# Row sums of a fourth of the attention heads: from matrix multiplications to accumulating transfers, with a reordered program

## The chip, the core and the metric

The kernel runs on one core of a Trainium2 chip. The core has five engines that work side by side, each through its own list of instructions in order: PE (TensorE, matrix multiplications), DVE (VectorE), ACT (ScalarE), POOL (GpSimd) and SP (SyncE, which here only starts transfers). They meet by semaphores: an instruction waits until what it reads is written and what it overwrites is no longer read. 16 DMA engines carry transfers, which POOL and SP start. The metric is the device time of one launch in microseconds (us).

## What is computed

The reference is two graph layers over 32 graphs of 512 nodes with 256 features, 8 heads of 32, everything in float32:

```python
# layer 0, then layer 1 without the feed-forward part; x is (32, 512, 256)
allowed = (adj > 0) | (adj.T > 0) | eye            # layer 1: adj != 0 alone
q, k, v = heads(x @ Wq.T + bq), heads(x @ Wk.T + bk), heads(x @ Wv.T + bv)
attn = softmax(where(allowed, q @ k.T / sqrt(32), -inf))
y = layernorm(x + (attn @ v) @ Wo.T + bo)          # layer 0
y = layernorm(y + relu(y @ W1.T + b1) @ W2.T + b2) # layer 0
x = layernorm(x + y)
```

The kernel does not subtract a row maximum. It computes p = exp(s) times the 0/1 mask, the product of p with v, and separately the row sum of p over the 512 keys, by whose reciprocal the product is multiplied. How this row sum is made is what the change is about.

## The kernel before, in words

**Layout.** Scores are held transposed, keys on the 128 partitions and queries along the row. The 512 keys are four chunks and the eight heads two head groups `hg` of four, so a layer of a graph has eight tiles `p(layer, k)`, k = 4 hg + chunk, each 128 x 4 heads x 512 queries. `scores(layer, k)` (L472) is eight small matmuls into the one PSUM tile `s`, `exp` (L487, ACT) turns it into p, `masked` (L490, DVE) multiplies p by the mask, and `product` (L494, PE) adds p times v to the one PSUM tile `acc`, which `context` (L507, ACT) copies to `cT`. Both layers share one `cT`, so `context` also waits for the `project` steps that read the last one.

**Row sums.** For each head group four p tiles are first folded into one, p(layer, 2 + hg):

- `pair(layer, k)` (L510) is an accumulating transfer started by POOL: p(k) += p(k + 1), 1024 KB. There are three in a layer.
- `fold` (L514) is an addition on DVE.

What is left is a sum over the 128 partitions of the folded tile. There are two ways, chosen by the set `SPREAD` (L164):

- `sums` (L517): four matmuls of the tile with a matrix of ones, on PE, into a PSUM bank. DVE then transposes the result in blocks (`blocks`, L558), takes the reciprocal (`invert`) of one column, transposes it back (`widen`) and multiplies (`divide`).
- spread: two accumulating transfers (`halve`, L536) add the upper half of the partitions to the lower half, 128 to 64 (512 KB) and 64 to 32 (256 KB); four `spread` transfers (64 KB each, started by SP) put the 32 rows of the four heads under each other in a tile `part`; `blocks` transposes `part`, and `reduce` (L566, DVE) adds 32 columns. `part` and its transpose have one buffer each. The rest is as above.

Before, the head groups (0, 0) and (1, 0), written (layer, hg), are spread, and (0, 1) and (1, 1) go over PE. Layer 0 of the first graph and layer 1 of the last are direct (L260): there all eight tiles are summed on PE, with no pair, fold, halve or spread.

**The rest of a graph.** `add`, `stats`, `aggregate` (DVE), `root` (POOL, two instructions), `center`, `affine`, `offset` (DVE) and `norm` (ACT) make the layer norms, numbered 1 to 4. `transpose` and `transpose_out` turn activations; `query_key`, `value`, `project`, `hidden` and `mlp` are dense matmuls, with `*_out` and `relu` on ACT taking them out of PSUM. A dense step is done as four 32-column matmuls side by side ("narrow", 128*32 in the profile) or as one of 128 columns (`wide=True`, 128*128); the values are the same. `flip`, `sort` and `join` bring x in transposed, `cast`, `entries` and `entry` bring the adjacency, `masks` makes the masks of it, and `guard` keeps a running sum of the totals for an overflow test at the end.

**The order.** Nothing is scheduled by a tool. Three lists written out by hand call these steps one by one, and each engine runs its share in that order: `opening` for graphs 0 to 4, `period` called 26 times, each with five consecutive graphs a to e, and `closing` for graphs 27 to 31. In a period, graph b is in its layer 1 attention, c in its layer 0 feed-forward part and norms, d in layer 0 attention, e is being loaded and a finished. Which buffer a tile gets is written out too, as strings of digits in `slots` (L168): three PSUM banks "d" for all dense results, eight buffers "p", and so on.

In the period of before, b.sums(1, 1) stands at L1725 behind d.product(0, 0), and b.blocks(1, 1) and b.invert(1, 1) a few steps behind it; the transfers of (1, 0) follow, with b.project(1, 0) at L1795.

Of the kernel before, what the change touches and what calls it, by code (L numbers as in the profile page):

```python
# [27 lines left out]
def kernel(ctx: ExitStack, tc: tile.TileContext, t: dict, out: bass.AP):  # L28
# [122 lines left out]
    def plain(pools: ExitStack):  # L151
# [7 lines left out]
        def dense(out, lhsT, rhs, start, stop, wide):  # L159

            for at in (slice(0, P),) if wide else [slice(j * HD, (j + 1) * HD) for j in range(HPC)]:
                nc.tensor.matmul(out[at], lhsT[:, at], rhs, start=start, stop=stop)  # L162

        SPREAD = {(0, 0), (1, 0)}  # L164
# [5 lines left out]
                "01201201010202020201212102110212101201202012020212010202102201201201201201011021021021021021102012102102102012012020"  # L170
                + "210212121020212121021021210210012121201202020121202020120120201201102020" * 13
                + "212120102112010201201202120121021101101221121221021202110210210210210120201201210120120120120120221212012012"
            ),
            "p": iter(
                "012345672103456712045673061537245024371652617403253074615261473065073142564213074"
                + "573021654162073153076245124673025073461526143076573014256421073453072165416273015073624512463072573046152614073653071425642173045073216541623071573062451246073253074615261473065073142564213074" * 2
                + "57301625465107352037416251467034273650124015673"
# [8 lines left out]
                + "101010" * 13  # L186
                + "1011101"
            ),
            "y": iter(
                "01230123012310320132013102130232131302312013010132102301"  # L190
                + "303012032130131302312013010132102301" * 8
                + "2003213012300303012301231010210213023102"
# [4 lines left out]
                + "011010100101"  # L197
            ),
            "st": iter(
                "01230132013201320132103213021302132013201203"  # L200
                + "12032103210321031230213021302130" * 13
                + "1203123021032103032103210321032103213021032103213201"
            ),
            "r": iter(
                "0123102101"
                + "31102001" * 13
                + "32212010123110"
# [7 lines left out]
                "01011001"  # L215
                + "1001" * 13
                + "1001"
            ),
            "total": iter(
                "01101"  # L220
                + "1001" * 13
                + "1000101"
# [439 lines left out]
        def opening(a, b, c, d, e):  # L662

            a.load()
            a.constants(0, 4)
            a.warm()
            b.flip(1)
            a.transpose(0, 0)
            a.transpose(0, 1)
            a.transpose_out(0, 0)  # L670
            a.cast(first[0])
            a.constants(22, 23)
            a.transpose_out(0, 1)
            a.query_key(0, 1, 0, None, wide=True)
            a.query_key(0, 0, 0, None, wide=True)
            a.query_key_out(0, 1, 0, None)
            a.query_key_out(0, 0, 0, None)
            a.scores(0, 2)
            a.exp(0, 2)
            a.entries()  # L680
            a.value(0, 1)
            a.scores(0, 1)
            a.exp(0, 1)
            a.query_key(0, 0, 1, None)
            a.query_key_out(0, 0, 1, None)
            a.entry(2)
            a.scores(0, 0)
            a.entry(0)
            a.exp(0, 0)
            a.entry(1)  # L690
            a.value(0, 0)
            a.entry(3)
            a.constants(6, 8)
            b.cast(first[6])
            a.value_out(0, 0)
            b.sort(1, 0, 0)
            a.masks(0)
            a.masks(1)
            a.scores(0, 3)
            a.query_key(0, 1, 1, None)  # L700
            a.masks(2)
            a.masked(0, 0)
            b.flip(0)
            a.masked(0, 2)
            a.constants(4, 6)
            b.sort(1, 0, 1)
            a.masked(0, 1)
            b.sort(1, 1, 0)
            a.exp(0, 3)
            a.masked(0, 3)  # L710
            a.query_key_out(0, 1, 1, None)
            a.scores(0, 4)
            b.sort(0, 0, 0)
            a.value_out(0, 1)
            a.exp(0, 4)
            a.masked(0, 4)
            b.sort(0, 1, 0)
            a.once(2, 0)
            a.once(2, 1)
            a.scores(0, 5)  # L720
            a.once(2, 2)
            a.once(2, 3)
            a.exp(0, 5)
            a.scores(0, 6)
            b.sort(0, 1, 1)
            a.masked(0, 5)
            a.exp(0, 6)
            a.product(0, 0)
            a.product(0, 1)
            a.product(0, 2)  # L730
            a.scores(0, 7)
            b.sort(1, 1, 1)
            a.exp(0, 7)
            b.sort(0, 0, 1)
            b.join(0, 0)
            a.product(0, 3)
            a.sums(0, 0)
            a.once(0)
            b.entries()
            b.join(1, 0)  # L740
            a.context(0, 0)
            b.entry(1)
            b.join(0, 1)
            a.product(0, 4)
            a.constants(12, 14)
            a.masked(0, 6)
            a.product(0, 5)
            a.masked(0, 7)
            a.constants(20, 22)
            a.product(0, 6)  # L750
            a.product(0, 7)
            a.blocks(0, 0)
            a.reduce(0, 0)
            a.constants(8, 10)
            a.sums(0, 1)
            a.constants(17, 20)
            a.once_out(0)
            a.context(0, 1)
            a.bias(1)
            b.join(1, 1)  # L760
# [3 lines left out]
            b.query_key(0, 0, 0, None)  # L764
            b.load()
            b.entry(3)
            c.flip(1)
            b.query_key_out(0, 1, 0, None)
            a.invert(0, 1)
            a.widen(0, 1)  # L770
            a.divide(0, 1)
            b.value(0, 0)
            b.query_key_out(0, 0, 0, None)
            a.invert(0, 0)
            a.widen(0, 0)
            b.entry(2)
            b.scores(0, 0)
            a.divide(0, 0)
            b.value_out(0, 0)
            a.project(0, 0)  # L780
            a.project(0, 1)
            b.exp(0, 0)
            b.scores(0, 1)
            a.add(1, 1)
            a.stats(1, 1)
            a.add(1, 0)
            c.cast()
            a.stats(1, 0)
            a.aggregate(1, 1)
            a.add(1, 3)  # L790
            a.aggregate(1, 0)
            a.once(1)
            a.constants(10, 12)
            b.exp(0, 1)
            a.center(1, 1)
            a.once_out(2)
            a.stats(1, 3)
            b.query_key(0, 1, 1, None, wide=True)
            a.masks(3)
            a.root(1, 0, 2)  # L800
            a.add(1, 2)
            a.stats(1, 2)
            a.affine(1, 1)
            a.center(1, 0)
            a.affine(1, 0)
            b.query_key(0, 0, 1, None, wide=True)
            a.aggregate(1, 2)
            b.query_key_out(0, 1, 1, None)
            a.transpose(1, 0)
            b.entry(0)  # L810
            b.masks(0)
            a.aggregate(1, 3)
            a.center(1, 3)
            b.query_key_out(0, 0, 1, None)
            a.transpose_out(1, 0)
            a.root(1, 2, 4)
            b.scores(0, 2)
            a.hidden(0, 2)
            a.affine(1, 3)
            c.flip(0)  # L820
            a.relu(0, 2)
            a.once_out(1)
            a.hidden(0, 4)
            c.entry(1)
            c.sort(0, 1, 0)
            c.sort(0, 0, 0)
            a.hidden(0, 0)
            a.relu(0, 3)
            b.exp(0, 2)
            c.sort(0, 1, 1)  # L830
            b.masks(1)
            a.relu(0, 4)
            a.relu(0, 5)
            b.masks(2)
            b.scores(0, 3)
            b.exp(0, 3)
            a.center(1, 2)
            a.affine(1, 2)
            b.masked(0, 0)
            a.relu(0, 1)  # L840
            a.transpose(1, 1)
            b.value(0, 1, wide=True)
            b.value_out(0, 1)
            b.bias(1)
            b.masked(0, 2)
            b.scores(0, 5)
            b.masked(0, 1)
            b.product(0, 0)
            b.pair(0, 0)
            b.masks(3)  # L850
            c.join(0, 1)
            a.hidden(0, 6)
            c.sort(1, 1, 0)
            b.exp(0, 5)
            a.relu(0, 0)
            a.guard(0, 0, 1)
            b.masked(0, 3)
            c.entry(2)
            b.masked(0, 5)
            b.product(0, 1)  # L860
            b.product(0, 2)
            b.pair(0, 2)
            a.relu(0, 7)
            a.transpose_out(1, 1)
            a.hidden(1, 2)
            a.bias(0)
            a.relu(0, 6)
            a.mlp(0)
            a.mlp(1)
            a.add(2, 0)  # L870
            a.stats(2, 0)
            a.aggregate(2, 0)
            b.bias(0)
            a.relu(1, 3)
            a.hidden(1, 4)
            a.relu(1, 2)
            c.sort(1, 1, 1)
            c.join(1, 1)
            c.sort(0, 0, 1)
            b.product(0, 3)  # L880
            a.add(2, 1)
            a.stats(2, 1)
# [2094 lines left out]
```

## Time and profile before

| | us |
|---|---|
| median of 3 runs (2986.01 to 2986.1) | 2986.01 |
| the profiled execution | 2986.66 |
| its span, first to last instruction | 2984.9 |
| TensorE clock granted, share of full | 0.999 |
| one of the 26 periods | 91.58 |
| opening, up to the first period's first matmul | 304.7 |
| psR matmuls (all sums), 624 records | 79.8 busy |
| p<-p transfers in the software queue with the mask's | 47.5% of 16 engines' span |

Busy time of an engine is the union of its instructions. A matmul in float32 is two records, and its end is modelled and lies in the next one's time, so the time that a step takes on PE is read from its start to the start of the next. In the tables "x512" is a count, "busy, mean ns" the time of a group, and what stands behind the next bar is idle time of the engine ahead of the group, with what ended it. A tile's name is without its number: psR is a bank of `sums`, acc of `product`, psO of `project`, psF of `mlp`, psH of `hidden`, psT of `transpose`, s of `scores`. L162 is the helper through which all dense matmuls go.

### The profile page before, as it was taken

The numbers are of one execution on the slowest core, as the hardware profiler recorded it, in microseconds if no ns is written. First come the engines' busy times: TensorE is split into PE (matmuls) and PEld (weight loads), VectorE is DVE, ScalarE is ACT, GpSimd is POOL, SyncE is SP. The second block draws the span as 40 slices with busy tenths as digits, with TensorE's granted clock in tenths as the row PEclk, the third lists the DMA queues.
The fourth block names the chain that finished last, engine by engine and source line by source line (L and its number), as shares of the span: only waits on it lengthen the run. The fifth ranks groups of instructions, "written<-read, shape, count | busy, mean of one in ns | idle before, by whom it ended". The sixth has DMA issues, their size and how long they took to land.

```text
span 2984.9 us, 83822 instructions
## 1 busy us (share of the span) xinstructions
PE 2959.3 (99%) x36852; PEld 1369.0 (46%) x36852; DVE 2700.2 (90%) x3585; ACT 1748.9 (59%) x2111; POOL 1002.0 (34%) x1247
## 2 busy tenths in 40 slices
PE   9999999999999999999999999999999999999997
PEld 4444444454444444444544445444445444454443
DVE  5889999999999999999999999999999999998996
ACT  5555665655665556655566555566555665656554
POOL 0333333332333323333323333233332333333332
PEclk9999999999999999999999999999999999999999
DMA  7566766776666667667676766676676766767551
GB/s 174 109 115 129 156 130 134 135 127 137 133 135 135 122 132 147 134 128 136 129 144 127 133 134 130 131 143 131 131 132 128 146 130 133 135 123 141 100 109 29
DMA packets 276436, 387.08 MB, mean 130 GB/s; under 512 B 153248, under 2 KB 237344, under 8 KB 245792
## 3 DMA queue, kind: packets, MB, share of 16 engines
q0 software_dynamic: 35744, 260.59, 47.5%
q1 hardware_dynamic: 240320, 121.05, 18.4%
q8 instruction: 291, 4.77, 0.6%
q14 instruction: 81, 0.66, 0.1%
HBM read 72.23 MB, written 33.55 MB: 35 GB/s over the span
## 4 chain that ended last, share of the span: by engine, by line
PE 95%; DVE 2%; ACT 1%; DMA 1%; issue 0%; POOL 0%; SPq 0%; DVEq 0%; POOLq 0%
PE s L479 18%; PE acc L499 15%; PE psH L162 15%; PE psF L162 15%; PE psQK_None L162 11%; PE psV L162 7%; PE psO L162 7%; PE psQK L162 4%; PE psT L440 2%; PE psR L523 2%; ACT p L488 1%; DMA p<-p 1%; DVE st L606 0%; DVE p L515 0%; DVE y L603 0%
## 5 line engine op out<-in xcount | busy, mean ns | idle before, releaser
L488 ACT ACTIVATE p<-s 128x2048 f32<-128x2048 f32 x512 | 963.6, 1882 | 486.0 <-PE s L479 478.7
L492 DVE TENSOR_TENSOR p<-p,m 128x2048 f32<-128x2048 f32 x512 | 1162.5, 2278 | 29.7 <-ACT p L488 26.5
L479 PE MATMUL s<-qT,kT 32*64 32x512 f32 x8192 | 570.4, 613 | 6.8 <-ACT p L488 2.7
L499 PE MATMUL acc<-p,v 128*32 128x512 f32 x4096 | 507.8, 595 | 0.0
L162 PE MATMUL psH<-xT,w_L_gnn_W 128*32 128x256 f32 (+1 forms) x6296 | 471.0, 380 | 0.0
L162 PE MATMUL psF<-w_L_gnn_W,hT 128*32 128x256 f32 (+1 forms) x6896 | 459.9, 379 | 0.0
L614 POOL TENSOR_SCALAR rs<-mv 128x2 f32<-128x2 f32 (+1 forms) x320 | 215.2, 673 | 684.4 <-DVE mv L609 664.8
L515 DVE TENSOR_TENSOR p<-p,p 128x2048 f32<-128x2048 f32 x186 | 424.3, 2281 | 3.9 <-DMA p<-p 2.7
L162 PEld LDWEIGHTS psH<-xT,w_L_gnn_W 128*32 128x32 f32 (+1 forms) x6296 | 300.3, 118 | 199.5 <-issue 54.7
L615 POOL TENSOR_TENSOR rs<-rs,neg_half 128x2 f32<-128x2 f32 (+1 forms) x320 | 369.8, 1156 | 26.7
L162 PEld LDWEIGHTS psF<-w_L_gnn_W,hT 128*32 128x32 f32 (+1 forms) x6896 | 286.6, 115 | 184.7 <-ACT hT L650 31.4
L512 POOL DMA_DIRECT2D p<-p x186 | 171.3, 921 | 497.8 <-PE acc L499 435.4
L650 ACT ACTIVATE hT<-psH,c_L_gnn_b 128x256 f32<-128x256 f32 x512 | 212.5, 475 | 193.5 <-PE psH L162 184.4
L479 PEld LDWEIGHTS s<-qT,kT 32*64 32x64 f32 x8192 | 119.2, 129 | 313.5 <-issue 109.3
L539 POOL DMA_DIRECT2D p<-p x124 | 106.4, 858 | 443.7 <-DVE mv L609 193.5
L162 PE MATMUL psQK_None<-xT,w_L_gnn_Wqkv 128*32 128x512 f32 (+1 forms) x1988 | 243.1, 594 | 0.7 <-ACT xT L445 0.7
L162 PE MATMUL psO<-w_L_gnn_Wo,cT 128*32 128x256 f32 (+1 forms) x2728 | 240.0, 380 | 2.7 <-DVE cT L585 2.7
L499 PEld LDWEIGHTS acc<-p,v 128*32 128x32 f32 x4096 | 118.7, 109 | 256.7 <-issue 193.0
L162 PEld LDWEIGHTS psO<-w_L_gnn_Wo,cT 128*32 128x32 f32 (+1 forms) x2728 | 154.5, 123 | 97.8 <-issue 43.0
L445 ACT COPY xT<-psT 128x512 f32<-128x512 f32 x130 | 76.1, 586 | 199.4 <-PE psT L440 199.4
L635 ACT ACTIVATE x<-z,ms,rs 128x256 f32<-128x256 f32 x128 | 73.5, 599 | 158.6 <-DVE ms L619 155.4
L606 DVE BATCH_NORM_STATS2 st<-y 128x6 f32<-128x256 f32 x384 | 155.0, 422 | 6.5
(79 smaller groups left out, 2873.9 us busy)
## 6 DMA issues: line engine op xcount, KB each, us to landing
p<-p POOLq DMA_DIRECT2D x186, 1024.0 KB, 7.8
p<-p POOLq DMA_DIRECT2D x62, 512.0 KB, 5.9
x<-in_x_dram SPq DMA_DIRECT2D x32, 512.0 KB, 4.2
code<-in_adj_dram POOLq DMA_DIRECT2D x32, 512.0 KB, 6.3
m<-code SPq DMA_DIRECT2D x32, 512.0 KB, 4.9
kT<-v SPq DMA_DIRECT2D x248, 64.0 KB, 4.0
p<-p POOLq DMA_DIRECT2D x62, 256.0 KB, 5.9
part<-p SPq DMA_DIRECT2D x248, 64.0 KB, 2.0
```

The source lines that it names most:

```text
L162: nc.tensor.matmul(out[at], lhsT[:, at], rhs, start=start, stop=stop)
L479: nc.tensor.matmul(s[half * P // 2 : (half + 1) * P // 2, j, :], self.kT(layer)[at, hg, key : key + P // 2], self.qT(layer)[at, hg, :], st ...
L488: nc.scalar.activation(self.p(layer, k), self.at("s", (layer, k), [HPC, N]), AF.Exp, scale=SCALE)
L492: nc.vector.tensor_tensor(p, p, m[:, k % NQ, None, :].to_broadcast([P, HPC, N]), ALU.mult)
L499: nc.tensor.matmul(acc[j * HD : (j + 1) * HD, :], self.v(layer)[:, kc, h * HD : (h + 1) * HD], self.p(layer, k)[:, j, :], start=(kc == 0), ...
L512: nc.gpsimd.dma_start(out=self.p(layer, k), in_=self.p(layer, k + 1), accum_op=ALU.add)
L515: nc.vector.tensor_tensor(self.p(layer, dst), self.p(layer, a), self.p(layer, b), ALU.add)
L539: nc.gpsimd.dma_start(out=p[:rows], in_=p[rows : 2 * rows], accum_op=ALU.add)
L606: nc.vector.bn_stats(self.at("st", (n, i), [6]), self.y(n, i))
L614: nc.gpsimd.tensor_scalar(rs, self.mv(n)[:, a:b, 1:2], EPS, None, ALU.add)
L615: nc.gpsimd.tensor_tensor(rs, rs, neg_half[:, a:b, None], ALU.pow)
L650: nc.scalar.activation(self.hT(h)[:, f, :], ps[:, f % 2, :], AF.Relu, bias=b1[:, f : f + 1])
```

## The change

1. `SPREAD` gains (1, 1). Layer 1's second head group is now summed by two `halve` and four `spread` transfers and a `reduce`, in all graphs but the last; its `sums` step on PE goes.
2. The period is written in another order: the same steps for the same five graphs, but for item 1, with other neighbours and partly other offsets between the graphs. Five dense steps of the period go from wide to narrow and four from narrow to wide.
3. The opening and the closing are rewritten to lead into the new period and out of it, and the strings of `slots` with them.

The diff, cut to its core, with the new period's steps that the sum of (1, 1) touches:

```diff
-        SPREAD = {(0, 0), (1, 0)}
+        SPREAD = {(0, 0), (1, 0), (1, 1)}
...
         slots = {
             "d": iter(
-                "01201201010202020201212102110212101201202012020212010202102201201201201201011021021021021021102012102102102012012020"
...
+                "01201201212020202021020121012021210120120212210102010121100201201210120120120202202120202010210210210121021021020200"
...
         def period(a, b, c, d, e):
...
-            b.sums(1, 1)
...
-            b.blocks(1, 1)
...
-            b.invert(1, 1)
...
```

The new period around them, other steps left out:

```python
c.halve(0, 0, P // 2)
c.halve(0, 0, P // 4)
c.spread(0, 0, 0)
...
c.fold(0, 3, 3, 4)
c.sums(0, 1)
...
b.masked(1, 0)
b.product(1, 0)
...
a.root(4, 0, 2)
c.blocks(0, 1)
...
c.divide(0, 0)
...
c.project(0, 1)
...
c.project(0, 0)
...
b.context(1, 0)
b.scores(1, 6)
...
b.product(1, 4)
...
b.masked(1, 6)
...
b.pair(1, 4)
c.root(1, 0, 2)
...
c.affine(1, 0)
...
c.center(1, 1)
c.affine(1, 1)
...
c.transpose(1, 0)
c.transpose_out(1, 0)
d.scores(0, 0)
...
b.fold(1, 3, 6, 7)
...
b.fold(1, 3, 3, 4)
...
c.hidden(0, 0)
...
b.halve(1, 1, P // 2)
...
b.halve(1, 1, P // 4)
b.halve(1, 0, P // 2)
...
b.spread(1, 1, 0)
...
b.spread(1, 1, 3)
...
b.spread(1, 1, 1)
b.halve(1, 0, P // 4)
...
d.scores(0, 4)
d.exp(0, 4)
...
b.spread(1, 1, 2)
...
d.masked(0, 4)
...
c.root(2, 0, 2)
...
e.entry(1)
b.blocks(1, 1)
...
b.reduce(1, 1)
...
b.spread(1, 0, 2)
...
b.invert(1, 1)
b.widen(1, 1)
...
b.divide(1, 1)
...
b.blocks(1, 0)
b.reduce(1, 0)
...
b.project(1, 0, wide=True)
...
b.project(1, 1, wide=True)
...
d.scores(0, 7)
d.context(0, 0)
d.product(0, 4)
...
c.scores(1, 2)
```

In the new opening, where graph 0 is still alone on the engines, the steps around the fourth to sixth scores are:

```python
a.scores(0, 3)
...
a.exp(0, 3)
a.value(0, 0)
...
a.scores(0, 6)
...
a.exp(0, 6)
...
a.scores(0, 4)
...
a.product(0, 0)
```

## The prediction

> **What bounds the kernel.** I read the shares of busy time first, then the chain that ended last:
>
> ```profile
> PE 2959.3 (99%) x36852; PEld 1369.0 (46%) x36852; DVE 2700.2 (90%) x3585; ACT 1748.9 (59%) x2111; POOL 1002.0 (34%) x1247
> PE 95%; DVE 2%; ACT 1%; DMA 1%; issue 0%; POOL 0%; SPq 0%; DVEq 0%; POOLq 0%
> ```
>
> PE is the path nearly everywhere, so a step taken from PE is worth its time on PE, unless the new order makes PE wait. Since matmuls overlap, I take a step's cost from start to start. The timeline of PE in one period (start, length, engine, line, tiles, count):
>
> ```profile
> 1169.84 1.04 PE L499 MATMUL acc<-p,v 128*32 128x512 f32 x8
> 1170.81 1.11 PE L479 MATMUL s<-qT,kT 32*64 32x512 f32 x16
> ...
> 1176.49 0.66 PE L440 MATMUL psT<-ident,x 128*128 128x128 f32 x4
> 1176.98 3.62 PE L162 MATMUL psF<-w_L_gnn_W,hT 128*128 128x256 f32 x16
> 1180.53 1.11 PE L479 MATMUL s<-qT,kT 32*64 32x512 f32 x16
> 1181.58 1.07 PE L499 MATMUL acc<-p,v 128*32 128x512 f32 x8
> 1182.46 1.04 PE L523 MATMUL psR<-p,ones 128*32 128x512 f32 x8
> 1183.32 1.91 PE L162 MATMUL psH<-xT,w_L_gnn_W 128*32 128x256 f32 x32
> ```
>
> Here sums(1, 1) costs 1183.32 - 1182.46 = 0.86 us. A product costs 0.86 to 0.88 before another narrow step and 0.97 before scores (1170.81 - 1169.84): 0.114 more. From the same view over all periods: a narrow step ahead of scores or of a transpose pays 0.114, a wide step ahead of them 0.094, a transpose ahead of anything but a wide step 0.093; every other neighbour pays 0.00 to 0.03. The second timeline row shows nothing of the kind behind scores.
>
> The windows view gives one period (length, then busy us of PE, PEld, DVE, ACT, POOL):
>
> ```profile
> 1128.93:1220.51 91.58, 91.58 (x1125) 42.93 (x1117) 84.74 (x113) 54.62 (x67) 33.77 (x42) 1.00 0.68 133
> ```
>
> PE never pauses in it, at full clock (1.00). DVE is idle for 91.58 - 84.74 = 6.84 us, so it is the next bound.
>
> **The sums that leave PE.** 31 of 32 graphs lose sums(1, 1) (the last graph adds layer 1 directly): 31 x 0.86 = 26.7 us.
>
> **The new order on PE.** Counted over both lists, narrow steps ahead of scores or transposes go from 429 to 450, wide ones from 117 to 96, transposes ahead of anything but wide from 17 to 39: 21 x 0.114 - 21 x 0.094 + 22 x 0.093 = +2.5 us. Wide and narrow cost the same otherwise (a hidden step 1.73 either way). In a period this makes 91.6 - 0.86 + 0.11 = about 90.8.
>
> **What DVE, POOL and SP gain.** DVE gets reduce(1, 1) where invert read the transposed sums directly; its row (busy, mean ns | idle before):
>
> ```profile
> L568 DVE TENSOR_REDUCE total<-sT 128x16 f32<-128x512 f32 x62 | 42.5, 686 | 2.0
> ```
>
> 0.69 us and a 0.03 gap; blocks reads SBUF, 0.70 instead of 0.72. DVE then needs 85.4 of 90.8 us and keeps 5.4 idle: still under PE, if its waits are not worse than now. POOL gets two accumulating issues (0.92 and 0.87 busy), SP four issues of 0.59; all lie beside PE (POOL 34 of 91 us). The cost of the transfers is when they land (KB, median us to landing):
>
> ```profile
> p<-p POOLq DMA_DIRECT2D x62, 512.0 KB, 5.9
> ...
> p<-p POOLq DMA_DIRECT2D x62, 256.0 KB, 5.9
> part<-p SPq DMA_DIRECT2D x248, 64.0 KB, 2.0
> ```
>
> **Does PE wait in the new period?** I laid the new list's PE steps end to end with these durations (scores(1, 2), its last step, ends at 90.8, which is 0 of the next) and walked the places where another engine is close.
>
> *The new chain.* product(1, 4) of b ends at 21.4; pair(1, 4) is issued some 0.5 later and lands 7.8 after that (its row's median), at 29.7. DVE reaches fold(1, 3, 3, 4) at about 30.2 and ends it at 32.5. First halve: 32.7 to 38.6; second, held on POOL until then, lands at 44.6; four spreads, three in a row on SP and the fourth behind them, land by 49.6. DVE reaches blocks(1, 1) at 54.2, since masked(0, 4) before it waits for exp(0, 4), whose scores end at 49.9. Margin 4.6 us. Behind the second halve POOL holds halve(1, 0) and root(2, 0, 2), which is not due before 52; behind the spreads SP holds d's mask transpose and the sorts, whose joins are due from 53 on: covered. The Trainium skill ("DMA: Bandwidth & Descriptors", Anatomy of one DMA) fits 2.0 us plus bytes / 436e3 to such a transfer: 3.2 and 2.6, so 5.8 for both halves where the rows give 11.8. I take the rows; by the rule the margin would be 10.6 instead of 4.6. The slowest landings of this trace (9.4 twice, 7.2 for a spread) would take 12.2 more and break it: PE time is then lost.
>
> *part is one buffer.* Layer 1's second use waits for blocks(1, 1), done at 54.9; its four spreads land by about 60 and blocks(1, 0) comes at 63.8.
>
> *Start of the period.* exp(1, 2) ends at 2.05. From there DVE has masked(1, 2), (1, 3), (1, 4) at 2.2 each, blocks to divide of (0, 1) 2.3, of (0, 0) 3.1, small ones 0.3 and a wait for root(4, 0, 2) of some 0.6: divide(0, 0) ends at 14.9. project(0, 1) needs it at 15.9: margin 0.8 with 0.2 for the signal.
>
> *First norm.* This is where a rule speaks against the change: the skill ("GPSIMD Engine Reference", Specifications) says that GpSimd shares its SBUF interfaces with VectorE, with contention when a DVE instruction has two SBUF inputs. masked and fold are such. The trace agrees:
>
> ```profile
> 1125.06 2.38 POOL L614 TENSOR_SCALAR rs<-mv 128x2 f32<-128x2 f32 x1
> 1127.52 2.70 POOL L615 TENSOR_TENSOR rs<-rs,neg_half 128x2 f32<-128x2 f32 x1
> ...
> 1195.76 0.22 POOL L614 TENSOR_SCALAR rs<-mv 128x2 f32<-128x2 f32 x1 [1.26 <-DVE mv L609]
> 1196.06 0.72 POOL L615 TENSOR_TENSOR rs<-rs,neg_half 128x2 f32<-128x2 f32 x1
> ```
>
> A root takes 5.1 us beside masked(1, 0) and fold, 0.9 beside small ones. The new root(1, 0, 2) starts at about 22.5, as masked(1, 6) runs (22.7 to 24.9, held by exp(1, 6)). By the fast row it ends at 23.5 and costs nothing; by the rule it crawls until 24.9 and ends near 26.1, affine(1, 1) ends at 27.6, and transpose(1, 0) is due at 28.75: still 0.9 to spare. I take the rule, and no stall.
>
> *ACT.* Three hand-overs are tighter than before. context(1, 0) starts 0.11 after project(0, 0) has let go of cT (so now in the trace), takes 0.59, and PE needs about 0.26 after ACT's end: 0.96, with one scores step of 1.04 to cover it. Twice the same, for context(0, 0) and for transpose_out(1, 0) ahead of hidden(0, 0). Between 0 and 0.1 us each; taken as 0, since 0.08 covers them.
>
> The end of DVE's walk lies some 3 us ahead of the next period, so nothing builds up. PE already waits 0.08 per period at a bank hand-over of query_key; one such place remains: no change.
>
> **Both ends.** In the opening, scores(0, 6) now stands directly ahead of scores(0, 4); starts of scores are held 3.15 us apart by exp there (14.83 after 11.68 on PE), of which scores fill 1.05, so 2.1 us of PE are bare. The old opening lost about 0.8 at its place: +1.4, say 2. In the closing one project step less fills the last graph's exp-bound stretch: between 0 and 2, taken as 1 (nearer to neither, the gap being partly bare already).
>
> **Sum.** -26.7 + 2.5 + 2 + 1 = -21.2. The profiled execution took 2986.66 (span 2984.9 and 1.8 around it), the median 2986.01 to 0.7 below it: 2965.5 and 2964.8. Forecast **2965 us**.
>
> **Rivals.**
> 1. *Part of it is lost on ACT's hand-overs and the ends*: three places at 0.1 us x 31 = 9, so 2974. For it: margins of 0.08. Against: PE's waits for ACT in the whole old run sum to under 10 us.
> 2. *Slower: the sums arrive late.* One mechanism: the two halves and four spreads of (1, 1) land behind the other transfers (DMA share 0.68 already, about 0.75 afterwards), blocks(1, 1) waits at the head of DVE's queue, and all norms behind it move with it. It decides from 4.6 us late; by the walk DVE then has about 1.5 us before a projection or transpose of PE is held up, and each further us costs 31. At 7.2 us late in every period it is 7.2 - 4.6 - 1.5 = 1.1, so 34 us and 2999; break-even is at 4.6 + 1.5 + 21/31 = 6.8 us late. For it: the slowest landing of 9.4. Against: the median of 5.9 and a fastest of 4.5.
> 3. *Nothing gained*: PE now has the order's idle instead of the sums, 2986. For it: DVE at 94% of the new period. Against: the walk.
>
> **Chances.** Forecast 0.58, first rival 0.17, second 0.18, third 0.07. What tells from no change is 0.2%, 6 us: faster 0.75, same 0.07, slower 0.18. The range 2957 to 2989 holds the forecast with the unknown ends, rivals 1 and 3.
>
> **What would show it.** PE's row for the period: 90.8 with PE at full busy time; psR matmuls down by 248; no wait of PE on DVE in the periods; DVE's wait for part near zero and POOL's halve held for about 6. Wrong if the period stands at 91.6 or more, or PE shows waits on cT, xT or acc each period.

## The result, and the profile after

The changed kernel takes 2975.04 us (median of 5 runs, 2968.85 to 2982.66), the kernel before 2986.01: a ratio of 0.9956, 95% interval 0.9943 to 0.9969. It is faster by 0.44%, where 2965 us, 0.70%, was forecast. The profiled execution took 2975.04, its span is 2972.9. A later set of 12 runs of the same kernel gave a median of 2978.35, from 2971.07 to 2986.57, beside 2987.31 for the kernel before: 0.31% faster. So the gain is 0.3 to 0.4%, about half of what was forecast, and the runs of the changed kernel differ by up to 15 us, which has to be explained too.

The page of the kernel after, busy time and chain:

```profile
PE 2936.9 (99%) x35800; PEld 1381.0 (46%) x35800; DVE 2706.8 (91%) x3617; ACT 1734.8 (58%) x2111; POOL 917.8 (31%) x1309
PE 90%; DVE 4%; DMA 2%; ACT 1%; issue 1%; SPq 1%; POOL 0%; DVEq 0%; ACTq 0%; POOLq 0%
```

PE is busy 22.4 us less, but the span fell by only 12.0. The chain says where to look: PE's share went from 95% to 90%, and DMA, SP's queue and DVE came in. DMA issues (KB, median us to landing):

```profile
p<-p POOLq DMA_DIRECT2D x93, 512.0 KB, 7.0
p<-p POOLq DMA_DIRECT2D x93, 256.0 KB, 4.8
part<-p SPq DMA_DIRECT2D x372, 64.0 KB, 2.5
```

93 instead of 62 halves of each size: the transfers of (1, 1) are there. The two medians together are still 11.8 us, as in the rows of before. The windows view of three of the 26 periods, numbers 8, 9 and 16 (stretch, length, busy us of PE, PEld, DVE, ACT, POOL, granted clock, DMA share, GB/s):

```profile
947.92:1038.69 90.77, 90.77 (x1116) 42.72 (x1108) 84.90 (x114) 54.12 (x67) 32.91 (x41) 1.00 0.77 147
1038.69:1131.33 92.64, 91.01 (x1116) 42.76 (x1108) 84.91 (x114) 54.34 (x67) 28.93 (x41) 1.00 0.76 143
1675.97:1771.29 95.32, 92.69 (x1117) 43.95 (x1109) 85.04 (x114) 54.34 (x67) 27.89 (x41) 0.98 0.80 139
```

24 of the periods are like the first: 90.77 us, PE never idle. Numbers 9 and 16 are 1.87 and 4.55 longer.

To see where the rest is, I added up every PE step at its undisturbed start-to-start time and took this sum from the length that the trace shows. The split is this calculation, not a view; the slow clock told of below counts as a wait:

| us | before: sum of steps | before: waits | after: sum of steps | after: waits |
|---|---|---|---|---|
| opening | 297.3 | 6.3 | 299.4 | 12.0 |
| 26 periods | 2378.2 | 3.0 | 2360.4 | 6.1 |
| closing | 277.3 | 8.4 | 268.2 | 13.2 |
| together | 2952.8 | 17.7 | 2928.1 | 31.3 |

The steps became 24.7 us cheaper and the waits 13.6 us longer, which leaves 11.1 of the 12.0 us by which the span fell; the last us lies after the last project. The question is what these 13.6 us are.

**The two long periods.** Over the whole run PE and DVE waited as follows (us in total, times, longest):

```profile
PE psO L162 <- DVE cT L585: 10.1, 4, 4.9
```
```profile
DVE sT L564 <- DMA part<-p: 9.7, 4, 3.3
```

So PE stood at project for `divide`, and DVE at `blocks` for the spreads. Not all of it is in the periods: of PE's four waits, 1.6 us are in period 9, 2.6 in period 16, 4.9 in the opening and 1.0 in the closing; of DVE's, 2.3 are in period 9 and 3.3 in period 16. In period 16 they are (DVE, then PE):

```profile
1733.62 0.71 DVE L564 STREAM_TRANSPOSE sT<-part 128x512 f32<-128x512 f32 x1 [3.31 <-DMA part<-p]
1747.03 5.16 PE L162 MATMUL psO<-w_L_gnn_Wo,cT 128*128 128x256 f32 x15 [2.63 <-DVE cT L585]
```

From start to start PE's pause is 2.8 us there, against 1.8 in period 9; this measure, some 0.16 longer than the idle time in the bracket, is used from here on. SP's timeline in period 16 (start, us, line, tiles, count; L418 is `flip`, the flip(1) of graph e first and then its flip(0); L423 is `sort`, L544 `spread`):

```profile
1704.82 5.49 SPq L418 DMA_TRANSPOSE v<-in_x_dram  x1
1715.70 1.41 SPq L423 DMA_DIRECT2D kT<-v  x2
1717.15 4.25 SPq L418 DMA_TRANSPOSE v<-in_x_dram  x1
1726.34 2.76 SPq L423 DMA_DIRECT2D kT<-v  x2
1729.26 2.83 SPq L544 DMA_DIRECT2D part<-p  x4
```

and in period 8, from flip(0) on:

```profile
985.36 1.31 SPq L418 DMA_TRANSPOSE v<-in_x_dram  x1
988.80 1.73 SPq L423 DMA_DIRECT2D kT<-v  x2
992.00 3.91 SPq L544 DMA_DIRECT2D part<-p  x4
```

In period 8 flip(0) is issued in 1.31 us and sort(0, 0, 0), which waits for its landing, follows 3.4 us after its start; the spreads of (1, 1) go out 44.1 us into the period, when their halves have landed. In period 16 both flips are slow (5.49 and 4.25 to issue), sort(0, 0, 0) can only follow 9.2 us after flip(0) began, and the spreads go out at 53.3, though their second halve was issued at 39.6 and had landed at 44.5, as in the other periods (issued at 38.8 to 40.3, landed by 45.0). The last spread lands near 57.6, `blocks(1, 1)` was due at 54.3: DVE waits 3.3 us and PE 2.8.

**The halved clock.** The remaining 1.76 us of period 16 are no wait. Windows of PE's pause and of the 3.4 us behind it, first in the opening, then in period 16:

```profile
192.60:197.60 5.00, 0.15 (x3) 0.07 (x1) 4.76 (x11) 1.50 (x1) 0.00 (x0) 0.98 1.06 218
197.40:200.80 3.40, 3.24 (x8) 2.64 (x9) 2.34 (x9) 0.00 (x0) 2.11 (x5) 0.50 0.23 46
1743.90:1747.00 3.10, 0.50 (x4) 0.26 (x3) 2.97 (x7) 1.88 (x1) 0.00 (x0) 1.00 1.01 206
1747.05:1750.40 3.35, 3.35 (x8) 2.70 (x9) 2.16 (x8) 0.00 (x0) 2.18 (x5) 0.50 1.04 213
```

After a pause of 2.8 and one of 5.0 us PE runs at clock 0.50 for 3.4 us, so the wide project step that follows takes 1.7 us longer. The page's clock row, in slices of 74 us, shows a 9 everywhere. The 1.8 us pause of period 9 brought no drop; which pauses do is worked out in the last section.

**The opening.** It is 7.8 us longer. Steps and the 2.1 us bare ahead of scores(0, 4), which had been forecast, are a part; the larger one is the pause of 5.0 us at 192.6 and its 1.7 us of slow clock. ACT just ahead of it:

```profile
181.70 1.92 ACT L650 ACTIVATE hT<-psH,c_L_gnn_b 128x256 f32<-128x256 f32 x5
187.94 0.78 ACT L430 COPY xT<-kT 128x512 uint16<-128x512 uint16 x1 [4.31 <-DMA kT<-v]
188.58 1.86 ACT L488 ACTIVATE p<-s 128x2048 f32<-128x2048 f32 x1
```

`join(1, 0)` (L430) waits 4.31 us for a sort, and exp(0, 5), masked(0, 5), the divisions and project queue up behind it. The sort was issued on SP at 183.2: SP had stood at the spreads of (1, 1) until 171.7, with all eight sorts of the graph behind them.

### The profile page after: what moved, and what is told of

Read it like the earlier page. It is cut to its first block, busy times and chain, and to the rows that moved or that the text cites. A ratio compares the mean times of both kernels' runs of the same rounds, so it can differ in the third digit from the quotient of the medians.

```text
span 2972.9 us, 82379 instructions
## 1 busy us (share of the span) xinstructions
PE 2936.9 (99%) x35800; PEld 1381.0 (46%) x35800; DVE 2706.8 (91%) x3617; ACT 1734.8 (58%) x2111; POOL 917.8 (31%) x1309
## 3 DMA queue, kind: packets, MB, share of 16 engines
q0 software_dynamic: 39712, 284.98, 54.2%
## 4 chain that ended last, share of the span: by engine, by line
PE 90%; DVE 4%; DMA 2%; ACT 1%; issue 1%; SPq 1%; POOL 0%; DVEq 0%; ACTq 0%; POOLq 0%
PE s L479 17%; PE acc L499 14%; PE psH L162 13%; PE psF L162 13%; PE psQK_None L162 11%; PE psO L162 7%; PE psV L162 7%; PE psQK L162 4%; PE psT L440 2%; PE psR L523 1%; DVE p L492 1%; ACT p L488 1%; DMA p<-p 1%; DMA v<-in_x_dram 1%; SPq L544 0%
## 5 line engine op out<-in xcount | busy, mean ns | idle before, releaser
L499 PE MATMUL acc<-p,v 128*32 128x512 f32 x4096 | 519.4, 597 | 1.1 <-DVE p L492 0.5
L162 PE MATMUL psF<-w_L_gnn_W,hT 128*32 128x256 f32 (+1 forms) x5264 | 453.6, 379 | 0.0
L614 POOL TENSOR_SCALAR rs<-mv 128x2 f32<-128x2 f32 (+1 forms) x320 | 195.2, 610 | 805.1 <-DVE mv L609 790.2
L539 POOL DMA_DIRECT2D p<-p x186 | 154.7, 873 | 753.1 <-DMA p<-p 566.2
L162 PEld LDWEIGHTS psF<-w_L_gnn_W,hT 128*32 128x32 f32 (+1 forms) x5264 | 322.0, 125 | 131.2 <-issue 11.5
L162 PEld LDWEIGHTS psH<-xT,w_L_gnn_W 128*32 128x32 f32 (+1 forms) x7400 | 272.6, 113 | 233.4 <-issue 65.8
L512 POOL DMA_DIRECT2D p<-p x186 | 168.7, 954 | 391.7 <-DVE st L606 234.7
L615 POOL TENSOR_TENSOR rs<-rs,neg_half 128x2 f32<-128x2 f32 (+1 forms) x320 | 262.6, 821 | 26.7
L650 ACT ACTIVATE hT<-psH,c_L_gnn_b 128x256 f32<-128x256 f32 x512 | 204.9, 478 | 91.2 <-PE psH L162 91.2
L508 ACT COPY cT<-acc 128x512 f32<-128x512 f32 x128 | 75.0, 586 | 114.2 <-PE psO L162 105.6
L162 PEld LDWEIGHTS psQK_None<-xT,w_L_gnn_Wqkv 128*32 128x32 f32 (+1 forms) x2012 | 63.7, 110 | 158.6 <-issue 139.2
```

Source lines behind the costliest of these rows:

```text
L499: nc.tensor.matmul(acc[j * HD : (j + 1) * HD, :], self.v(layer)[:, kc, h * HD : (h + 1) * HD], self.p(layer, k)[:, j, :], start=(kc == 0), ...
L512: nc.gpsimd.dma_start(out=self.p(layer, k), in_=self.p(layer, k + 1), accum_op=ALU.add)
L539: nc.gpsimd.dma_start(out=p[:rows], in_=p[rows : 2 * rows], accum_op=ALU.add)
L614: nc.gpsimd.tensor_scalar(rs, self.mv(n)[:, a:b, 1:2], EPS, None, ALU.add)
L615: nc.gpsimd.tensor_tensor(rs, rs, neg_half[:, a:b, None], ALU.pow)
L650: nc.scalar.activation(self.hT(h)[:, f, :], ps[:, f % 2, :], AF.Relu, bias=b1[:, f : f + 1])
```

## The experiments

My theory was one cause for these places: **head of line on SP**. The spreads share one queue with the flips and sorts of a coming graph; whichever waits holds up the other. The first rival was that the halves themselves land late, which the landings above already speak against; others were that the new order, and not the transfers, brings the gain (or that it only makes room), and that the loss lies elsewhere in the ends.

### The order of SP in the period

```diff
-            e.flip(0)
...
-            e.sort(0, 0, 0)
...
             b.spread(1, 1, 2)
+            e.sort(1, 0, 1)
+            e.flip(0)
...
             b.spread(1, 0, 3)
+            e.sort(0, 0, 0)
+            e.sort(0, 0, 1)
+            e.join(0, 0)
```

All steps with a plus leave their old places. `join(0, 0)`, which reads these sorts on ACT, moves with them; the rest of the kernel is the same.

> The changed kernel's period with SP's queue alone in another order: the second flip of the next graph and its sorts (0,0,*) stand behind the spreads of (1,1) and (1,0) instead of ahead of them. Theory (the two long periods of the changed kernel come from a slow flip at the head of SP, with spread(1,1,*) queued behind it): all 26 periods 90.77 us, no wait of TensorE for cT inside the periods, so 1.87 + 4.55 = 6.4 us less than the changed kernel's profiled 2975.0 with the same opening, about 2969, and less difference from run to run. Rival (the halving transfers themselves land late): one or more periods are still 2 to 5 us long, with the spreads issued late although nothing slow stands ahead of them, about 2975.

Measured: 2969.32 us (6 runs, 2968.45 to 2970.35), ratio 0.9936, 0.9923 to 0.9948. All 26 periods at once, from the windows view:

```profile
313.20:2673.30 2360.10, 2360.10 (x28818) 1110.85 (x28813) 2207.74 (x2939) 1409.49 (x1717) 757.80 (x1066) 1.00 0.78 146
```

That is 26 periods of 90.77, with no gap of PE. And SP in its period 16:

```profile
1703.62 5.49 SPq L418 DMA_TRANSPOSE v<-in_x_dram  x1
1714.37 3.71 SPq L423 DMA_DIRECT2D kT<-v  x3
1719.16 3.77 SPq L544 DMA_DIRECT2D part<-p  x4
```

The first flip is as slow as before (5.49), but the spreads now go out at 44.4 us of the period. The runs differ by 1.9 us instead of 14. The theory holds for the periods, and the halves are cleared: with the slow flip out of the way, the first spread left at 43.6 to 45.0 in every period. The opening kept its pause (5.4 us) and its slow clock.

### The transfers undone, the new order kept

```diff
-            b.halve(1, 1, P // 2)
...
-            b.halve(1, 1, P // 4)
...
-            b.spread(1, 1, 0)
...
             d.product(0, 2)
+            b.sums(1, 1)
...
+            b.blocks(1, 1)
+            b.reduce(1, 1)
             b.invert(1, 1)
```

Here (1, 1) goes over PE again in the 26 periods, and the other three spreads go too, and `blocks` and `reduce` move from their old places; opening and closing stay.

> The changed kernel's order with the transfers of (1,1) undone in the 26 periods: halve, spread and part(1,1) go, sums(1,1) is back on TensorE behind product(0,2) and blocks(1,1) reads its bank. Theory (the gain is the 0.86 us of these matmuls in each period): period 90.77 + 0.86 = 91.63, 26 x 0.86 = 22.4 us more, less the 6.4 us of the two long periods, which need the spreads: about 2991 (2986 to 2997). Rival (the new order, not the transfers, brings the gain): period near 90.8 and about 2970.

Measured: 3007.74 us (6 runs). Every odd period took 91.63, every even one 92.67. The extra 1.04 stood between sums(1, 1) and mlp(2), and it came from my own edit: the strings of buffers cover two periods with banks 0 and 2 exchanged, and in every second one I had given sums the bank that mlp(2) needs next. With the free bank in each:

> The run with sums(1,1) back on TensorE again, with the bank that is free in each of the two periods of the pattern (in the first try the bank was the busy one in every second period, which waited 1.0 us). Theory: all periods 91.63, 3007.7 - 13 x 1.04 = 2994. Rival (something else lengthens every second period): they stay at 92.67.

Measured: 2995.49 us (9 runs), all periods 91.63, ratio 1.0031, 1.0021 to 1.0041. From the windows view, two periods:

```profile
1000.00:1183.26 183.26, 183.26 (x2234) 86.17 (x2233) 169.25 (x227) 108.25 (x132) 54.40 (x78) 1.00 0.69 133
```

183.26 = 2 x 91.63. So the transfers are worth 91.63 - 90.77 = 0.86 us a period, to the hundredth what the sums cost on PE. The new order gains nothing by itself: with the sums on PE its period is 91.63, against 91.58 before. (The whole kernel is slower than the one before, but it still has the transfers of (1, 1) in the opening and the closing, and a drop of the clock in each.)

### The transfers alone, in the old order

```diff
             c.affine(1, 2)
+            b.fold(1, 3, 3, 4)
...
             b.halve(1, 0, P // 4)
+            b.halve(1, 1, P // 2)
...
             c.root(2, 0, 2)
+            b.halve(1, 1, P // 4)
...
             e.sort(0, 0, 0)
+            b.spread(1, 1, 0)
...
             def sums(self, layer, hg):
+                if (layer, hg) == (1, 1) and 2 <= self.b <= 27:
+                    next(slots["d"])
+                    return
```

The last part takes the matmuls of (1, 1) out of the periods and leaves the sequence of PSUM banks as it was.

> The transfers of (1,1) alone, in the order of the kernel before, in the 26 periods: fold(1,3,3,4) goes up behind affine(1,2) (from 49.7 to 46.5 us in the period), the halves follow on GpSimd, the spreads stand behind sort(0,0,0) on SP, and (1,0) and (1,1) change places in blocks, invert, widen and divide. By the rows of the kernel before the halves land at about 55.5 and 61 and the spreads at 66, where blocks(1,1) stands at 66.6 and the projection at 73.6: about 3 us of margin. Theory (the reorder isn't what pays; it only makes room): if that walk holds, period 91.57 - 0.86 + 0.05 = 90.76, opening and closing as before, 2986 - 26 x 0.81 = 2965. Rival (the old order has no room, so the new order is needed): the spreads come over 3 us late, the projection waits, period 91.6 or more and 2986 or more.

Measured: 3054.16 us (5 runs), ratio 1.0207, 1.0184 to 1.0230; periods of 92.7 to 101.6. My walk failed: in a typical period the spreads went out from 61.8 us on, the last at 65.1, took 4.1 to 5.8 us to land where I had used 2.0, and `blocks(1, 1)` came at 69.9 instead of 66.6. Behind it on DVE stood offset(3, 0, 2), which norm(3, 0) and so transpose(2, 0) wait for: no room where I had seen 3 us. A second try took that out of the way:

> The run with the transfers of (1,1) in the old order again, with all four spreads of (1,0) ahead of sort(0,1,0) on SP, and with root(3,0,2), offset(3,0,2) and add(2,2) ahead of blocks(1,1), so that only the divisions and project(1,1) wait for the spreads. If it was the queue behind blocks(1,1) on VectorE that made 93.1 us, the period falls to 91.0 to 91.6 and the time to between 2970 and 2986. If the old order lacks the room in any case (halves and spreads land at 70, divide(1,1) ends at 73.3, the projection starts at 73.6), it stays above 92 and 2995.

Measured: 3067.83 us (4 runs), worse again. The wait at transpose(2, 0) was gone, but up to 2.5 us stood at transpose(2, 1), and the clock halved 18 times in the run. Both were my placements, so this doesn't prove that the old order could not take the transfers with other placements; it shows that two plain attempts lost 2 to 3%.

### The opening

First, two of the sorts moved up, and exp(0, 5) ahead of the join:

```diff
+            d.sort(1, 0, 0)
+            d.sort(1, 0, 1)
             d.sort(1, 1, 0)
...
+            c.exp(0, 5)
             d.join(1, 0)
```

> The changed kernel with the opening alone mended: d.sort(1,0,*) stand ahead of entry(1), sort(0,0,1) and load on SP, and exp(0,5) ahead of join(1,0) on ScalarE. Theory (the 5.0 us wait at 197 us is ScalarE's join(1,0) waiting for a sort that SP issued late, and the 1.7 us behind it are the granted clock that fell to 0.5 after the wait): both go, the opening takes 304.7 us instead of 311.4, no clock record of 0.5 near 200 us, about 2968.5 if the periods are as in the profile of the changed kernel. Rival (something else is late there too, such as the spreads of (1,1) or the divisions): the wait only moves, the opening stays over 309.

Measured: 2973.96 us (6 runs, 2966.53 to 2984.33). The pause shrank from 5.0 to 0.5 us and the clock stayed up there, but 2.0 us came back at mlp(2), since join(1, 1) now waited for its later sort; the opening took 4.3 us less, not 6.7. In the profiled run periods 9 and 16 were long again, 96.66 and 95.27, which hid the gain. Then, with the period's SP order, all four sorts ahead of the spreads:

```diff
+            d.sort(1, 0, 0)
+            d.sort(1, 1, 0)
+            d.sort(1, 1, 1)
+            d.sort(1, 0, 1)
             a.spread(1, 1, 0)
```

> The kernel with SP's order changed in the period, and in the opening the four sorts (1,*,*) of the fourth graph ahead of the spreads of (1,1), which stand at the head of SP until their halves have landed. Theory (what the opening lost is the same head of line, seen through ScalarE's joins): the wait of 5 us ahead of the first project(1,0) and the 1.7 us of halved clock behind it go, opening 312 -> 305, periods 90.77, 2969.3 - 7 = 2962. Rival (the opening has another limit close behind, as in the run with only two of these sorts moved, where 2.0 us came back at mlp(2)): opening over 308, about 2966 or more.

Measured: **2962.85 us** (5 runs, 2961.77 to 2963.74), ratio 0.9914, 0.9899 to 0.9928. The opening took 6.1 us less than in the run with the period's order alone, no clock record of 0.5 lies before the end of the run, and all periods are 90.77. This version beats both kernels.

### The closing

> The kernel with both SP changes, and in the closing fold(1,3,3,4) of the fourth graph with its halves and spreads behind affine(1,2) of the fifth, and its blocks(1,1) to invert(1,1) behind affine(2,2). Theory (in the closing the fold and the blocks of (1,1) stand on VectorE ahead of what transpose(1,1) and transpose(2,0) wait for, 1.45 and 1.6 us): both waits go, closing 283.1 -> 280.3, 3 us under the kernel with the opening alone mended. Rival (the divisions of (1,1) come too late for project(1,1), which waits as long as was won): no gain, or up to 3 us lost.

Measured: 2969.71 us (6 runs), 6.9 us more than without the edit. The wait at transpose(1, 1) went, but the one at transpose(2, 0) grew from 1.8 to 6.5 us and brought a slow clock (10.2 us of it). SP and ACT of the better kernel, the one without this edit, show why:

```profile
2893.88 0.59 SPq L660 DMA_DIRECT2D out_dram<-x  x1
```
```profile
2897.10 1.09 ACT L635 ACTIVATE x<-z,ms,rs 128x256 f32<-128x256 f32 x2 [3.99 <-DVE r L573]
```

norm(3, 1) (L635) writes a buffer that the store of an earlier graph still reads, and that store stands on SP behind the spreads of (1, 1), which my edit had made later. The view names DVE's reciprocal, which ended at 2897.05 and is the semaphore that came last; the store landed at 2897.02, which fits as well. To tell, from the better kernel:

```diff
+            e.root(1, 2, 4)
             d.halve(1, 1, P // 2)
-            e.root(1, 2, 4)
...
+            c.store()
             d.spread(1, 1, 1)
...
-            c.store()
```

> The kernel with both SP changes, and in the closing two queue places alone: the store of the third graph ahead of the spreads of (1,1) on SP, and root(1,2,4) ahead of the 64-row halve on GpSimd. Theory (norm(3,1) of the fifth graph writes the tile that this store reads; the store is issued at 2893.9 behind four spreads and norm starts 3.2 us later, as it started 3.1 us after the store before the change; and the root waits behind a halve that waits for its fold): the waits of 1.8 us at transpose(2,0) and of 1.4 us at transpose(1,1) go, closing 283.8 -> 280.6, 2959.6. Rival (norm(3,1) waits for invert(1,1), as the view of waits names it): transpose(2,0) still waits about 1.8 us, at best 1.4 us are won, 2961.4 or more.

Measured: 2962.66 us (5 runs, 2962.43 to 2964.7), as without it. ACT in that run:

```profile
2892.24 0.84 ACT L650 ACTIVATE hT<-psH,c_L_gnn_b 128x256 f32<-128x256 f32 x2 [0.52 <-PE psH L162]
2892.98 1.09 ACT L635 ACTIVATE x<-z,ms,rs 128x256 f32<-128x256 f32 x2
```

norm(3, 1) now follows at once, though the reciprocal still comes later (2897.79): the store it was, and the wait at transpose(2, 0) is gone. But transpose(1, 1) waits 2.0 instead of 1.4, and project(1, 1) 1.7 instead of 0.6. The 1.8 us were handed on, and the early root did not help transpose(1, 1). What bounds the closing stays open.

### The changed kernel once more

> The changed kernel once more, beside the mended ones. If the long periods come with certain graphs (the input of the 13th and the 20th flips slowly in both profiles that have this order), periods 9 and 16 are the long ones again, and the runs differ by some 10 us; if the slow flips fall at random, other periods are long. Median between 2969 and 2977.

Measured: 2978.35 us (12 runs, 2971.07 to 2986.57), ratio 0.9969, 0.9956 to 0.9981; the kernel of the last run, with both places mended and the store moved, took 2962.66 beside it with a width of 2.3. The median is above what I expected. Period 16 was long again (92.83), period 9 was not. In the three profiles with this order of SP flip(1) takes about 5 us in periods 2, 5, 9, 16, 22 and 26, in the others mostly 3.5 to 4.8, so slow flips come back at the same graphs, or the same places in the run, which these runs can't tell apart; in these profiles a stall came only when the second flip was slow too (3.2 to 4.3 us, in periods without a stall 1.3 to 2.4).

## Why the prediction was right, and where it was short

- *The sums that leave PE, 0.86 us each*: right. Undoing them costs 0.86 a period.
- *The new neighbours on PE, +2.5*: the steps became 24.7 us cheaper together, so it was 26.7 - 24.7 = 2.0. The period was given as about 90.8 and is 90.77; the difference is mostly the wait of 0.08 us at query_key, which the walk kept and which is gone (0.94 us from that step to the next before, 0.86 now).
- *The walk*: right wherever nothing stood in the way. Period 8, forecast and measured: the first halve issued at 32.7 and 33.4, the spreads landed by 49.6 and 49.4, `blocks(1, 1)` at 54.2 and 54.25, `blocks(1, 0)` at 63.8 and 63.78, divide(0, 0) ends at 14.9 and 15.2. DVE has 84.90 us of work where 85.4 was said.
- *Rows against the rule for the halves*: from the first issue to the second landing (1, 1)'s own two halves took 10.3 to 11.8 us in the 26 periods, 10.9 in the median. The rows' 11.8 was a little long; the rule's 5.8 was about half.
- *The slow root*: I took the contention rule, and root(1, 0, 2) took 3.2 us and ended at 26.2 where 26.1 was said. affine(1, 1) followed in time.
- *ACT's hand-overs*: 24 periods without any wait of PE, so that part of the first rival is out. Its 2974 is the figure nearest to the measured 2975.04, but by luck: all 9 us of it were hand-overs, which cost nothing. Its other part, the ends, is where half of the miss and more lies: 3 us of waits were taken for both, and they grew by 5.7 and 4.9.
- *The failed step* is the sentence "behind the spreads SP holds d's mask transpose and the sorts ...: covered". It asks only what waits behind the spreads. Ahead of them on the same queue stood flip(0) and sort(0, 0, 0), and in the opening the sorts behind them had joins on ACT that came due earlier. This one omission is worth 6.4 us in the profiled periods and 6.1 in the opening, about the 12.2 us between 2975.04 and the 2962.85 of the kernel with both places mended. That this kernel lies even 2 us under the forecast is luck again: the closing's waits grew by 3.9 us more than the 1 that was taken for them, which stays open, and smaller terms of the other sign outweigh it, among them about 2 us of waits in the periods that the walk had kept.
- *The second rival* described the right symptom, `blocks(1, 1)` at the head of DVE waiting for part, with a wrong trigger (slow halves) and a wrong frequency (every period, where it was one or two). Its slack was too large: DVE 3.3 us late cost PE 2.8, and 2.3 cost 1.8, so 0.5 us instead of 1.5.
- *The signs*: psR fell by 248 records, to 376, as said. "No wait of PE on DVE in the periods" failed in two of 26, and DVE waited 9.7 us for part where near zero was said.
- *The price of a stall* was taken as its length. With the slow clock behind it, 2.8 us cost 4.55 and 5.0 cost 6.7.

## What to carry to other kernels

When work moves into transfers, walk the issuing queue in both directions: what stands ahead of the new transfer and may be held, and what stands behind it and is due while it waits. Put transfers that wait for something computed behind those that are ready, and slow prefetches behind both when there is time to spare. A spread of 10 us from run to run can be the sign of such a place: here, moving the slow flip off the queue's head lowered the median and brought the width from 14 us to 1.9.

## What the runs showed of the hardware

**The clock after a pause.** The Trainium skill ("TensorE: Matmul & The Clock Gate", Part 1: The HAM clock gate) says that TensorE falls to half its clock after an idle window of about 3.4 us, and that the window runs freely. The records here agree on the length: each drop lasts 3.413 us or two or three times that, but for the last one of a run, which lasts to its end. They agree that the window runs freely: in each of the nine profiles with more than one drop, all begin on one grid, whole multiples of 3.4133 us apart (in that of the changed kernel at 197.397 and 1747.048, 454 steps). They differ on how much must be idle.

Every pause of PE of 2.8 us or more brought a drop, of those between 2.0 and 2.8 some did (the bare 2.1 us ahead of scores(0, 4) in one profile of nine), and no single one under 2.0 did; one drop followed three waits of 0.4 to 0.7 us close together. The grid accounts for the in-between. I added up PE's idle time, as the profile has it, in each stretch of the grid that ran at full clock: of the 43 stretches with 1.95 us idle or more all were followed by a drop, of the 30 with 1.4 to 1.95 five, of over 10000 with less none. So somewhat more than half a stretch is enough here, and the same pause brings a drop or not by whether the grid cuts it in two. The clock came back after each slow stretch with 0.57 us idle or less and stayed down after each with 0.71 or more.

**The flips.** In the changed kernel a transposing transfer of the same 256 KB (half of one graph's x) took 1.25 to 5.49 us of SP to issue and landed in 3.2 to 10.9 us, where the kernel before had 1.25 to 3.58 and 3.3 to 9.0. Why some graphs flip slowly wasn't tried.
